# A two-block transformer on one core: inverses fetched in two transfers, three steps moved, two weight loads put later

## The chip, the cores and the metric

The kernel runs on one core of one Trainium2 chip. The metric is the device time of one execution in microseconds (us). It was run three times: median 2306.06 us, from 2299.68 to 2307.3. One further execution was taken by the profiler, and everything said of stages, lines and waits comes from that one.

The core has a matrix engine (TensorE; PE in the profile, its weight loads PEld), VectorE (DVE), ScalarE (ACT), GpSimd (POOL) and SyncE (SP). SyncE computes nothing here: it issues nearly all DMA transfers, in its program's order, and a transfer that has to wait for data holds up every later one on SyncE. Each engine works through its own instructions strictly in order.

## The reference

Everything is float32. The input x is 8 batch elements of 512 tokens by 256 features, with a condition vector per element and a context of 64 tokens by 192 features. Two transformer blocks follow each other.

```python
# block 0: 16 heads of 16
h = modulate(ln(x), shift_sa, scale_sa);  q, k = ln(heads(h)), ln(heads(h))
x = x + gate_sa * softmax(q k^T * scale) v
h = modulate(ln(x), ...);  x = x + gate_ca * (attention(h Wq, ctx) Wo + b)
h = modulate(ln(x), ...);  x = x + gate_ff * ((silu(h W1) * (h W3)) W2)
# block 1: 16 heads of 64, rotary position on q and k
x = attention(adaln(x), adaln(x)) Wo + b + x       # self-attention
x = attention(adaln(x), ln(context)) Wo + b + x    # cross-attention
x = gelu(adaln(x) W1 + b1) W2 + b2 + x
```

## The kernel before

All of x stays on the chip, one tile per batch element (`xs[b]`, 128 partitions by 4 by 256). Block 0 runs as cycles: `cycle(c)` lays the self-attention of element c beside the cross-attention of element c-1 and the feed-forward of element c-2. Block 1 runs stage by stage over the eight elements: self-attention (`slots`, in groups g = 0 to 3 of four heads), cross-attention (`cross`) and feed-forward (`feed_forward`). The order of every engine's instructions is the order in which these functions call each other: they run inside `tc.manual_schedule`, so nothing there is reordered. Only what stands outside of it, such as the two weight loads at lines 1226 and 1227, may be placed elsewhere in an engine's order when the kernel is built.

**Turned rows.** Matrix products need the normalized rows with the features on the partitions. A norm has three pieces: statistics of two row tiles each (twice, line 182 on; the second ends with `rstd` on GpSimd, line 158) and the application (line 191). Then `blocks_turned` (line 410) turns 32 by 32 blocks on VectorE (413), writes them to DRAM with four transfers (416, `turned_d`) and reads them back with one (418, into z). `modulated` (427) scales and shifts on ScalarE. A function `turn` calls it, some steps later. `add_row` (448) adds a bias row to x on GpSimd.

**Softmax denominators.** `sums` multiplies the exponentials by ones on TensorE, ScalarE copies the sums out (`den`), and SyncE sends them to DRAM and back so that they lie one per lane (`rec`; lines 1093 and 1095, or 1307 and 1309). `inverse` takes the reciprocal on VectorE, stores it (1101 or 1316) and fetches it back repeated over 64 partitions (`rb`; 1106 with 4 transfers, 1321 with 8, of 128 KB each). `scaled` multiplies by it on VectorE and GpSimd (1112 or 1328).

**Cross-attention of block 1.** `cross` starts with six queries, then has places j = 0 to 7 for each element b. At j = 0 and 4 come a `sums` and a `score`; at every j one `queries` call, six ahead: two products of 512 columns, and a rotation on VectorE (868, 869) that empties one of four PSUM banks used in rotation (`ps_D`, `ps_O`, two `ps_X`), and at every second j two sums on GpSimd (873, 874). At j = 0 and 1 `outer` multiplies the values by the output weights. For the element before: `scaled` for its first half at j = 0, `inverse` for its second half at j = 1, `scaled` at j = 4, and the output products `cross_out` at j = 5 to 7. At j = 1 `turn` modulates the next element's rows; at j = 2 keys and values of the next element are fetched; at j = 4, 5, 6 the three pieces of the norm of element b + 2 run (`rows_`), the last with `blocks_turned` and `add_row`; at j = 6, behind them, `inverse` for this element's first half. Element 0 has neither `outer` nor `cross_out` nor `scaled` among its places, so it is short.

**Weights.** `load_w` fetches 1 MB into one of the places of a pool. `ff_w1` goes to where `ca_wv4` was, `ff_w2` to where `sa_wo` was, which TensorE reads until the end of self-attention (`last_out`). Their first use is `up(0, ...)` in the last element of cross-attention, or the feed-forward.

Of the kernel before, what the change touches and what calls it, by code (L numbers as in the profile page):

```python
# [10 lines left out]
F32 = mybir.dt.float32  # L11
I32 = mybir.dt.int32
AF = mybir.ActivationFunctionType
ALU = mybir.AluOpType
# [3 lines left out]
B, N, D, H, T, CD, FF = 8, 512, 256, 16, 64, 192, 1024  # L18
P = 128
# [25 lines left out]
def fast_path(ctx: ExitStack, tc: tile.TileContext, a: dict, out: bass.AP):  # L45

    nc = tc.nc
# [71 lines left out]
    def row(name):  # L119
        lo, hi = _ROWS[name]  # L120
        return rows[:, lo:hi]
# [88 lines left out]
    wk = sa0.enter_context(tc.tile_pool(name="sa0", bufs=2, side="right"))  # L210
# [421 lines left out]
    class CrossAttention:  # L632
# [22 lines left out]
        def blocks(self):  # L655
            turned_blocks0(self)
# [144 lines left out]
    def cycle(c):  # L801

        s, nxt, prev = sa[c], of(sa, c + 1), sa[c - 1]
        x, done = ca[c - 1], of(ca, c - 2)
        up, down = of(ff, c - 2), of(ff, c - 3)
        keys = [lambda p=p: keys1(p) for p in range(NPAIR)] if c == 1 else [lambda: None] * NPAIR
        store = store_keys1 if c == 1 else lambda g: None
        late = [up.turn] if c == 2 else []
        soon, then = ([x.turn], []) if c == 1 else ([], [x.turn])
        rows2, rows3 = ([] if c < n else [s.blocks] for s, n in ((x, 2), (up, 3)))  # L810

        scores, values = of_self(s, 0)
# [4 lines left out]
        group(scores, [keys[2], lambda: store(0), lambda: down.down(1), lambda: x.prepare(0), lambda: x.prepare(1),  # L817
                       *([up.turn] if c > 2 else []), lambda: up.up(0), lambda: x.prepare(2), *rows2, keys[3], lambda: up.up(1)],
              [lambda: s.queries_keys(2), lambda: s.back(0), *soon, lambda: nxt.norm(2)], values)
# [173 lines left out]
    with tc.tile_pool(name="ph4", bufs=2, reuse_waits="tile") as wk:  # L993
# [4 lines left out]
        def by_way():  # L998
            return wk.tile([P, 2, N], F32, tag="t", name="t")

        class Batch:
# [6 lines left out]
            def norm(self, n):  # L1008
                self.pieces[n]()
                if n == 2:  # L1010
                    self.s["raw"] = blocks_turned(by_way(), self.s["z"])
                    add_row(self.b, row("sabo"))

            def turn(self):
                self.s["hT"] = modulated(rows_tile(nk), self.s["raw"], self.b, a1, b1)
# [81 lines left out]
            def inverse(self, g):  # L1097
                rec = self.s["rec", g]
                nc.vector.reciprocal(rec, rec)
                d = dram.tile([4, N], F32, tag="rec_d", name="rec_d")  # L1100
                nc.sync.dma_start(flat(d), rec)
                check(rec)
                for u in range(2):
                    self.s["rb", g, u] = rb = wk.tile([P, N], F32, tag="rb", name="rb", bufs=3)
                    for e in range(2):
                        nc.sync.dma_start(rb[64 * e : 64 * e + 64, :],
                                                d[2 * u + e : 2 * u + e + 1, :].to_broadcast([64, N]))

            def scaled(self, g):
                o = self.s["oT", g]  # L1110
                for u, eng in enumerate((nc.vector, nc.gpsimd)):
                    eng.tensor_tensor(o[:, u, :], o[:, u, :], self.s["rb", g, u], ALU.mult)

            def last_out(self, ks):
                s = self.s
# [16 lines left out]
        class First:  # L1132
# [4 lines left out]
            def norm(self, n):  # L1137
                self.pieces[n]()
                if n == 2:
                    first_rows.append(blocks_turned(by_way(), first_rows.pop()))  # L1140
                    add_row(0, row("cabo"))

            def turn(self):
                first_rows.append(modulated(rows_tile(nk), first_rows.pop(), 0, a1, b1))
# [3 lines left out]
        def slots():  # L1148
# [9 lines left out]
            for b, this in enumerate(todo):  # L1158
                nxt = todo[b + 1] if b + 1 < B else First()
                last = todo[b - 1] if b else None  # L1160
                for g in range(NG):
# [34 lines left out]
                    if before:  # L1196
                        before[0].scaled(before[1])
                    this.sums(g)
                    before = this, g
            end = todo[-1]  # L1200
            cross_values(wk, 1)
# [21 lines left out]

    extra.extend([bank_d, bank_o])
    with tc.tile_pool(name="ph5", bufs=2, reuse_waits="tile") as wk:
        w_f1 = load_w("ff_w1", 1)
        w_f2 = load_w("ff_w2", 3)
        kvs.append((wk.tile([P, NPAIR, T], F32, name="kb", bufs=1), wk.tile([P, NPAIR, 2, T], F32, name="vb", bufs=1)))


# [80 lines left out]
        def inverse(b, half):  # L1311
            s = ss[b]
            rec = s["rec", half]
            nc.vector.reciprocal(rec, rec)
            rd = dram.tile([4, 2, N], F32, tag="rec5", name="rec5")
            nc.sync.dma_start(flat(rd), rec)
            check(rec)
            for j in range(4):
                s["rb", j] = rb = wk.tile([P, N], F32, tag="rb", name="rb", bufs=4)
                for e in range(2):  # L1320
                    nc.sync.dma_start(rb[64 * e : 64 * e + 64, :], rd[j, e : e + 1, :].to_broadcast([64, N]))  # L1321

        def scaled(b, half):
            s = ss[b]
            for j in range(4):
                p = 4 * half + j
                pr = s["p", p // 2][:, p % 2, :]
                (nc.gpsimd, nc.vector)[p % 2].tensor_tensor(pr, pr, s["rb", j], ALU.mult)

        def out_tile(b, t, lhsT, w):  # L1330
            s = ss[b]
# [52 lines left out]
            return good  # L1384

        def cross():
            LEAD = 6
            held = [bank_s() for _ in range(2)]
            for n in range(LEAD):
# [4 lines left out]
            for b in range(B):  # L1394
                for j in range(NPAIR):
# [24 lines left out]
                    if j == 2 and b + 1 < B:  # L1420
                        load_kb(b + 1)
                        load_vb(b + 1)
                    if 3 < j < 7:
                        rows_(b + 2, j - 4)
                    if j == 6:
                        if b == B - 1:
                            sums(b, 1)
# [890 lines left out]
```

## Time and profile before

| | |
|---|---|
| median of 3 runs | 2306.06 us |
| the profiled execution | 2305.44 us |
| its span, first to last instruction | 2303.6 us |
| mean granted TensorE clock | 0.990 |
| TensorE busy | 2265.9 us, 98% |
| VectorE, GpSimd, ScalarE busy | 1124.5, 922.9, 865.9 us |
| DMA: bytes moved | 115.69 MB, mean 50 GB/s |
| rb<-rec_d, transfers | 128 of 128 KB (block 1 self-attention) |
| rb<-rec, transfers | 128 of 128 KB (block 1 cross-attention) |

Times are counted from the first instruction. Block 0 lasts to about 800 us, the self-attention of block 1 to 1751.5, its cross-attention to about 2069 and the feed-forward to the end. A line of the timeline has start, length, engine, line of the kernel, operation, output and inputs, and in brackets how long the engine was idle before it and what ended that wait. A "landing" is the time at which the last part of a transfer told that it had arrived.

### The profile page before, as it was taken

The numbers are of one execution on the slowest core, as the hardware profiler recorded it, in microseconds if no ns is written. First come the engines' busy times: TensorE is split into PE (matmuls) and PEld (weight loads), VectorE is DVE, ScalarE is ACT, GpSimd is POOL, SyncE is SP. The second block draws the span as 40 slices with busy tenths as digits, with TensorE's granted clock in tenths as the row PEclk, the third lists the DMA queues.
The fourth block names the chain that finished last, engine by engine and source line by source line (L and its number), as shares of the span: only waits on it lengthen the run. The fifth ranks groups of instructions, "written<-read, shape, count | busy, mean of one in ns | idle before, by whom it ended". The sixth has DMA issues, their size and how long they took to land.

```text
span 2303.6 us, 30880 instructions
## 1 busy us (share of the span) xinstructions
PE 2265.9 (98%) x12092; PEld 1145.7 (50%) x12092; DVE 1124.5 (49%) x1946; ACT 865.9 (38%) x1309; POOL 922.9 (40%) x584
## 2 busy tenths in 40 slices
PE   9999999999999999999999999999999899999999
PEld 4444554544545633535353535353535456567666
DVE  5676666665555345353535353545453555442220
ACT  4666455555542133342434242424241121221222
POOL 4652333333200056464646464645453444431110
PEclk9999999999999999999999999999999999999999
DMA  6120110101102001010101010101033333332221
GB/s 192 34 94 22 49 28 21 49 7 43 44 10 76 19 15 38 20 38 20 38 20 38 20 38 20 38 20 38 20 97 106 85 105 92 100 90 70 55 63 35
DMA packets 119819, 115.69 MB, mean 50 GB/s; under 512 B 40065, under 2 KB 93041, under 8 KB 119665
## 3 DMA queue, kind: packets, MB, share of 16 engines
q1 hardware_dynamic: 118800, 111.01, 16.9%
q8 instruction: 97, 1.59, 0.3%
q0 software_dynamic: 576, 2.10, 0.2%
q10 hardware_dynamic: 288, 0.52, 0.1%
q14 instruction: 58, 0.47, 0.1%
HBM read 85.73 MB, written 27.86 MB: 49 GB/s over the span
## 4 chain that ended last, share of the span: by engine, by line
PE 88%; DMA 4%; DVE 3%; SPq 2%; POOL 1%; issue 1%; ACT 0%; DVEq 0%; POOLq 0%; ACTq 0%
PE ps_P L88 40%; PE ps_B L88 30%; PE ps_S L88 5%; PE ps_D L88 4%; PE ps_X L88 4%; PE ps_O L88 2%; SPq L1321 1%; DMA rb<-rec 1%; DMA rec<-rec 1%; DMA turned_d<-hT 1%; PE ps_B L566 1%; SPq L416 1%; DVE z L191 1%; POOL var L557 1%; PE ps_B L598 1%
## 5 line engine op out<-in xcount | busy, mean ns | idle before, releaser
L615 ACT ACTIVATE p<-ps_B 128x512 f32<-128x512 f32 x576 | 291.6, 624 | 162.3 <-PE ps_B L88 162.2
L1058 ACT ACTIVATE p<-ps_P 128x1024 f32<-128x1024 f32 x256 | 244.9, 1025 | 90.0 <-PE ps_P L88 89.8
L88 PE MATMUL ps_P<-q,k 32*128 32x512 f32 x2048 | 238.9, 600 | 1.4 <-DVE t L1037 1.4
L1067 POOL TENSOR_TENSOR sm<-sm,p 128x1024 f32<-128x1024 f32 x64 | 176.9, 2764 | 135.3 <-ACT p L1058 134.7
L88 PE MATMUL ps_B<-hT,w 128*128 128x512 f32 x512 | 226.9, 597 | 1.4 <-ACT hT L407 0.9
L88 PE MATMUL ps_P<-p,v 128*32 128x512 f32 x2048 | 226.4, 594 | 0.0
L1026 ACT COPY v<-ps_P 128x1024 f32<-128x1024 f32 x32 | 32.4, 1012 | 375.8 <-PE ps_P L88 375.8
L1067 DVE TENSOR_TENSOR sm<-sm,p 128x1024 f32<-128x1024 f32 x64 | 101.6, 1588 | 145.3 <-ACT p L1058 145.3
L88 PEld LDWEIGHTS ps_P<-q,k 32*128 32x128 f32 x2048 | 99.1, 184 | 139.2 <-issue 113.6
L88 PEld LDWEIGHTS ps_B<-hT,w 128*128 128x128 f32 x512 | 95.3, 190 | 127.5 <-issue 97.0
L158 POOL TENSOR_TENSOR rstd<-rstd,mhalf 128x4 f32<-128x4 f32 x49 | 52.4, 1069 | 260.3 <-DVE rstd L157 259.1
L88 PE MATMUL ps_B<-q,k 16*128 16x512 f32 x1024 | 146.2, 618 | 1.2 <-DVE k L570 1.2
L88 PEld LDWEIGHTS ps_P<-p,v 128*32 128x32 f32 x2048 | 63.3, 110 | 158.3 <-issue 134.8
L1065 POOL TENSOR_TENSOR sm<-p 128x1024 f32<-128x1024 f32 x32 | 79.2, 2475 | 152.6 <-ACT p L1058 152.6
L557 POOL TENSOR_TENSOR var<-var,mhalf 128x32 f32<-128x32 f32 (+1 forms) x17 | 87.8, 5164 | 105.8 <-DVE var L551 98.8
L1036 DVE TENSOR_TENSOR t<-ps_P,rope_c 128x1024 f32<-128x1024 f32 x64 | 78.4, 1225 | 95.8 <-POOL q L1040 55.9
L88 PE MATMUL ps_B<-p,h 128*32 128x512 f32 x1024 | 120.5, 610 | 0.0
L609 POOL TENSOR_TENSOR attn<-attn,gate 128x256 f32<-128x256 f32 x32 | 23.4, 732 | 241.1 <-DVE attn L607 240.0
L1065 DVE TENSOR_TENSOR sm<-p 128x1024 f32<-128x1024 f32 x32 | 39.2, 1225 | 162.5 <-ACT p L1058 162.5
L88 PE MATMUL ps_P<-hT,w_sa_wq 128*128 128x512 f32 x256 | 118.3, 605 | 0.0
L88 PE MATMUL ps_B<-w,hid 128*128 128x256 f32 x512 | 115.4, 385 | 0.0
L88 PE MATMUL ps_P<-hT,w_sa_wk 128*128 128x512 f32 x256 | 115.1, 592 | 0.0
(246 smaller groups left out, 3708.3 us busy)
## 6 DMA issues: line engine op xcount, KB each, us to landing
z<-turned_d SPq DMA_DIRECT2D x35, 512.0 KB
rb<-rec_d SPq DMA_DIRECT2D x128, 128.0 KB
rb<-rec SPq DMA_DIRECT2D x128, 128.0 KB
turned_d<-hT SPq DMA_DIRECT2D x104, 128.0 KB
turned_d<-t SPq DMA_DIRECT2D x36, 128.0 KB
out_dram<-x SPq DMA_DIRECT2D x15, 256.0 KB
x<-in_x_dram SPq DMA_DIRECT2D x7, 512.0 KB
gate<-modd SPq DMA_DIRECT2D x24, 128.0 KB
```

Of the source, the lines that this page charges most:

```text
L88: nc.tensor.matmul(o, lhsT, rhs, start=start, stop=stop)
L158: nc.gpsimd.tensor_tensor(r[:, :n], r[:, :n], mhalf[:, :n], ALU.pow)
L191: nc.vector.tensor_scalar(d[:, t, :width], x[:, t, :], s["mv"][:, t, 0:1], s["r"][:, t : t + 1], ALU.subtract, ALU.mult)
L416: nc.sync.dma_start(d[:, :, :, r, :].rearrange("a j k c -> j k a c"), flat_[32 * r : 32 * r + 32].rearrange("j (k a c) -> j k a c", k=2, a=4))
L557: nc.gpsimd.tensor_tensor(var, var, half, ALU.pow)
L609: nc.gpsimd.tensor_tensor(attn, attn, gate.to_broadcast([P, NT, 4, HD0]), ALU.mult)
L615: nc.scalar.activation(p[i], ps, AF.Exp, scale=HD0 ** -0.5)
L1026: nc.scalar.copy(s["v", half][:, t0 : t0 + 2, :], ps)
L1036: nc.vector.tensor_tensor(c, ps, rope_c[:, None, :].to_broadcast([P, 2, N]), ALU.mult)
L1058: nc.scalar.activation(pr, pss[u], AF.Exp, scale=HD1 ** -0.5)
L1065: eng.tensor_tensor(s["sm", g, u], s["p", g, 0, u], s["p", g, 1, u], ALU.add)
L1067: eng.tensor_tensor(s["sm", g, u], s["sm", g, u], s["p", g, kt, u], ALU.add)
```

## The change

Five edits. (1) `inverse` in both attentions of block 1 fetches `rb` as one tile with two transfers, one for each half of the partitions, in place of four of 128 KB (self-attention) or eight (cross-attention): the bytes stay the same. (2) The rows of self-attention in block 1 are turned by a function of their own, `blocks`, called behind `sums(1)` and no longer in the third piece of the norm; `add_row` stays there. (3) In block 0 `rows2`, the turning of the rows for cross-attention, stands behind `up.up(1)` in the cycle's list. (4) In `cross` the three pieces of `rows_` move from j = 4, 5, 6 to j = 3, 4, 5. (5) `ff_w1` and `ff_w2` are loaded at j = 3 of the second element (b = 1), within the order written out by hand, and no longer before the stage.

```diff
 # cycle(c), group 1
-  ... lambda: up.up(0), lambda: x.prepare(2), *rows2, keys[3], lambda: up.up(1)],
+  ... lambda: up.up(0), lambda: x.prepare(2), keys[3], lambda: up.up(1), *rows2],
 # class Batch (class First likewise, with first_rows and "cabo")
             def norm(self, n):
                 self.pieces[n]()
                 if n == 2:
-                    self.s["raw"] = blocks_turned(by_way(), self.s["z"])
                     add_row(self.b, row("sabo"))
+
+            def blocks(self):
+                self.s["raw"] = blocks_turned(by_way(), self.s["z"])
 # Batch.inverse
-                for u in range(2):
-                    self.s["rb", g, u] = rb = wk.tile([P, N], F32, tag="rb", name="rb", bufs=3)
-                    for e in range(2):
-                        nc.sync.dma_start(rb[64 * e : 64 * e + 64, :],
-                                                d[2 * u + e : 2 * u + e + 1, :].to_broadcast([64, N]))
+                self.s["rb", g] = rb = wk.tile([P, 2, N], F32, tag="rb", name="rb")
+                for e in range(2):
+                    nc.sync.dma_start(rb[64 * e : 64 * e + 64], d[None, e::2, :].to_broadcast([64, 2, N]))
 # slots
                     this.sums(g)
+                    if g == 1:
+                        nxt.blocks()
 # before the stage
-        w_f1 = load_w("ff_w1", 1)
-        w_f2 = load_w("ff_w2", 3)
+        w_f1 = w_f2 = None
 # inverse of cross-attention
-            for j in range(4):
-                s["rb", j] = rb = wk.tile([P, N], F32, tag="rb", name="rb", bufs=4)
-                for e in range(2):
-                    nc.sync.dma_start(rb[64 * e : 64 * e + 64, :], rd[j, e : e + 1, :].to_broadcast([64, N]))
+            s["rb"] = rb = wk.tile([P, 4, N], F32, tag="rb", name="rb", bufs=1)
+            for e in range(2):
+                nc.sync.dma_start(rb[64 * e : 64 * e + 64], rd[None, :, e, :].to_broadcast([64, 4, N]))
 # cross, at place j of element b
-                    if 3 < j < 7:
-                        rows_(b + 2, j - 4)
+                    if 2 < j < 6:
+                        rows_(b + 2, j - 3)
+                    if b == 1 and j == 3:
+                        w_f1 = load_w("ff_w1", 1)
+                        w_f2 = load_w("ff_w2", 3)
```

In both `scaled` functions the operand `rb` becomes the matching slice of the one tile; otherwise they are the same.

More of the change, by code (lines that the diff above doesn't have):

```diff
@@ L817, in cycle @@
         group(scores, [keys[2], lambda: store(0), lambda: down.down(1), lambda: x.prepare(0), lambda: x.prepare(1),
-                       *([up.turn] if c > 2 else []), lambda: up.up(0), lambda: x.prepare(2), *rows2, keys[3], lambda: up.up(1)],
+                       *([up.turn] if c > 2 else []), lambda: up.up(0), lambda: x.prepare(2), keys[3], lambda: up.up(1), *rows2],
               [lambda: s.queries_keys(2), lambda: s.back(0), *soon, lambda: nxt.norm(2)], values)
@@ L1111, in scaled @@
                 for u, eng in enumerate((nc.vector, nc.gpsimd)):
-                    eng.tensor_tensor(o[:, u, :], o[:, u, :], self.s["rb", g, u], ALU.mult)
+                    eng.tensor_tensor(o[:, u, :], o[:, u, :], self.s["rb", g][:, u, :], ALU.mult)
             def last_out(self, ks):
@@ L1139, in norm, with blocks @@
                 if n == 2:
-                    first_rows.append(blocks_turned(by_way(), first_rows.pop()))
                     add_row(0, row("cabo"))
+            def blocks(self):
+                first_rows.append(blocks_turned(by_way(), first_rows.pop()))
             def turn(self):
@@ L1327, in scaled @@
                 pr = s["p", p // 2][:, p % 2, :]
-                (nc.gpsimd, nc.vector)[p % 2].tensor_tensor(pr, pr, s["rb", j], ALU.mult)
+                (nc.gpsimd, nc.vector)[p % 2].tensor_tensor(pr, pr, s["rb"][:, j, :], ALU.mult)
         def out_tile(b, t, lhsT, w):
@@ L1386, in cross @@
         def cross():
+            nonlocal w_f1, w_f2
             LEAD = 6
```

## Prediction, made before the result was known

> **What bounds the kernel now.** The page comes first. TensorE decides almost everywhere, so only the time in which it idles, or runs at half clock, can be won.
>
> ```profile
> span 2303.6 us, 30880 instructions
> PE 2265.9 (98%) x12092; PEld 1145.7 (50%) x12092; DVE 1124.5 (49%) x1946; ACT 865.9 (38%) x1309; POOL 922.9 (40%) x584
> ```
>
> Since busy matmul time is modelled, I read it by stretches next: length, then busy time of PE, PEld, DVE, ACT and POOL, granted clock, DMA share, GB/s. I cut at the end of block 1's self-attention (1751.5) and at each cross-attention element.
>
> ```profile
> 800.00:1751.50 951.50, 950.14 (x5681) 421.17 (x5681) 448.40 (x500) 340.19 (x372) 501.46 (x275) 1.00 0.12 36
> 1751.50:1791.50 40.00, 35.35 (x145) 15.81 (x143) 17.60 (x28) 8.21 (x11) 15.25 (x13) 0.91 0.21 47
> 1791.50:1839.70 48.20, 39.28 (x193) 22.94 (x192) 24.38 (x52) 8.70 (x12) 23.75 (x18) 0.93 0.34 90
> 1839.70:1878.07 38.37, 37.43 (x193) 22.52 (x192) 19.93 (x42) 8.81 (x12) 18.36 (x14) 1.00 0.37 99
> ```
>
> Self-attention of block 1 leaves PE 1.4 us idle in 951.5: nothing to win there. An undisturbed element is 37.4 us of PE. The first element (cut at 1791.5) idles 4.65 us, the second 8.92, the next five 0.94, 1.97, 1.04, 2.07 and 1.02 (the last four from the same view, not shown). The start of the feed-forward idles 0.79 more. Sum: 21.4 us. The waits of PE name the causes (total, times, longest):
>
> ```profile
> PE ps_D L88 <- DVE t L869: 13.9, 6, 6.8
> PE ps_X L88 <- DMA kv<-v_d: 4.6, 1, 4.6
> PE ps_X L88 <- ACT hT L427: 2.1, 1, 2.1
> ```
>
> For the 13.9 us, the chain of waits of a later element (start, length, what):
>
> ```profile
> 1839.10 0.33 SPq L418
> ...
> 1839.46 3.28 DMA rec<-rec
> ...
> 1847.18 3.10 DMA rb<-rec
> ...
> 1850.98 0.68 DVE t L868
> ...
> 1852.41 1.96 PE ps_D L88 x4
> ```
>
> SyncE holds the store of the inverses (L1316) until it has got past the turned rows (L418), then takes 4.96 us to issue eight transfers (L1321 from 1842.81 in the timeline); VectorE stands in `scaled` (L1328) until the last lands, the rotation of a query behind it comes late, and PE lacks the bank.
>
> Last, the clock, by stretches:
>
> ```profile
> 1754.22:1757.63 3.41, 0.89 (x3) 0.06 (x1) 1.79 (x3) 0.00 (x0) 1.05 (x1) 1.00 1.15 306
> 1757.63:1764.45 6.82, 4.69 (x8) 2.81 (x9) 0.00 (x0) 0.59 (x1) 1.43 (x2) 0.50 0.27 38
> 1808.83:1815.65 6.82, 3.20 (x4) 1.17 (x4) 3.93 (x8) 0.00 (x0) 3.75 (x3) 0.50 0.12 36
> ```
>
> After the two long gaps the granted clock is 0.50 for 6.82 us; what PE does in it takes twice as long. That costs half of the 4.69 us busy, 2.35, and 39.28 - 37.43 = 1.85 in the second element. With the idle time 25.6 us can be won at most.
>
> **Step 1, weights out of the opening.** SyncE's order there (start, length):
>
> ```profile
> 1743.22 0.55 SPq L140 DMA_DIRECT2D w_ff_w<-in_ff_w_dram  x1
> 1745.70 0.38 SPq L989 DMA_DIRECT2D v_d<-v  x1
> 1751.71 0.38 SPq L140 DMA_DIRECT2D w_ff_w<-in_ff_w_dram  x1
> 1752.15 1.25 SPq L977 DMA_DIRECT2D kv<-v_d  x2
> ```
>
> The first 1 MB load goes ahead of the store v_d<-v, which lands 6.44 us after its issue by the chain; another such store took 2.6 us alone (landing mark, issue 1716.93). The second waits for PE's last read of `sa_wo` and then goes ahead of kv<-v_d, which lands 6.84 us after its issue; the like load at 1777.46 took 3.0 and 4.0. Without the two: v_d<-v issued near 1744.5 (two issues fewer ahead of it, by step 2), landed by 1749, kv by 1754, and PE wants it at 1755.1, when its second query ends. The 4.65 us go, and with them the half clock, 2.35: **7.0 us**. Next late would be v_d<-v; if it lands as slowly as its slowest row (4.34), 1 us is left.
>
> **Step 2, two transfers for eight (four in self-attention).** One of the eight takes 0.6 us of SyncE whatever its form: the issues of L416 and L977, with more and shorter rows, take 0.62 to 0.67. So 4.96 becomes 1.25. The row for two 256 KB transfers is missing. Bounds: each lands 2.9 us after its issue, as 128 KB does (end 3.5 after the first issue), or they move like the 512 KB of z<-turned_d, 3.5, behind the second issue (4.1). Old: 7.5. I take 4.1, the nearer in bytes. A loss is excluded as long as they use all engines (rival 3).
>
> **Step 3, norms one j sooner.** In the code the norm's pieces go from j = 4, 5, 6 to 3, 4, 5: the same VectorE work (4 statistics, 4 applications of 0.35, a transpose of 1.25), `rstd` and `add_row` on GpSimd (1.0, 2.4) and five DMAs, all past one query and in later elements one output tile. SyncE's order stays: rows, then inverse. On GpSimd `rstd` comes right behind the multiplications of j = 4 and `add_row` behind a query's sums; nothing asks for either soon. In an undisturbed element, counted from its first matmul: the query of j = 5 ends at 21, rotation, norm and transpose at 25, the last L416 at 28, z is issued at 30 and lands at 33.4; VectorE's reciprocal stands at 31, so rec lands behind z at 33.5 and rb, by step 2, at 37.7. `scaled` asks at 37.4 + 6.2 = 43.6 (6.2 from 1839.70 to the end of the rotation before it). 6 us of slack, so the five gaps go, 0.94 + 1.97 + 1.04 + 2.07 + 1.02 = **7.0 us**, and the 0.79 of the feed-forward, whose last rb lands 3.4 sooner. GpSimd is next: 18.4 of 37.4 us busy, so it hides the move.
>
> The second element is not cured, for the first has no output tiles to cover anything. Normalized rows start after the rotation at 1789.47 instead of 1791.52, 2.05 sooner. The whole chain shifts: z lands 2.05 sooner and the 2.08 us wait for L427 goes. rec<-rec, still behind z<-turned_d, lands at 1800.7; rb at 1804.8 instead of 1810.1; two multiplications (1.4) and 1.4 until PE has its bank: 1807.6. PE ends its query at 1803.5: a gap of 4.1 stays of 8.9, 4.8 won. Half clock: gaps of 3.77 (at 693), 4.65 and 6.84 were followed by 6.8 us of it, 2.08 was not. So I expect it and charge 2.4, between nothing and 3.2 (6.39 us busy at 0.50 after the gap at 693, halved), against 1.85 now: **4.2 us** net. The Trainium skill, "TensorE: Matmul & The Clock Gate", Part 1, lets the clock halve after an idle window of about 3.4 us, with windows that run freely. By that a 4.1 us gap would hold a whole idle window only by luck of phase, and the sum would be 2.4 lower. The trace speaks against so strict a reading: the stretch 1754.22 to 1757.63 had 0.89 us of PE work, and 0.50 followed.
>
> **Step 4, the loads in the second element.** 1.0 us of SyncE and 2 MB, behind keys and values of the next element. The DMA engines reached 306 GB/s (stretch above), and 245 for the 1.5 MB from the second w_ff to kb, landed in 6.4 us: 7 to 9 us. Behind them on SyncE and its queue stand the element's own sums (den<-den, then rec<-den, which holds SyncE until they land) and the turned rows. Counted without the opening's 7 us, the sums land at 1823 to 1825, the reciprocal starts 0 to 1.6 us late on VectorE, with only rotations behind it, rb lands by 1837, and `scaled` asks at 1839. Forecast 0; bounds 0 and 8 (rival 1).
>
> **Step 5, turned rows behind sums.** Block 0: the transpose moves behind `up(1)`, two VectorE instructions, 1.3 us; L427 starts 2.5 to 4.7 us after z lands and ACT never idles before it. Block 1: blocks (one transpose, five DMAs) wait behind den_d<-den and its landing, 2 us; L427 has 6 us (1.8 in the first batch, where 0.3 may show on ACT, not on PE). den_d<-den goes 4.7 us sooner, and nothing asked for it. 0; without the slack 2 us a batch. The shorter rb of self-attention: VectorE and GpSimd waited once each for it (1.9, 2.5), under 14 us of PE's last products. 0.
>
> **Sum.** 7.0 + 4.2 + 7.0 + 0.8 = 19.0. The profiled execution took 2305.44 (span 2303.6), so 2286.4; the median shown is 0.6 above it: 2287.
>
> **Rivals.**
> 1. *The loads cost a gap.* If the 2 MB take 12.6 (twice the 6.3 of one), the second element's inverses land some 4 to 5 us late and a gap with half clock (3.2) comes between second and third: 8 us back, **2295**. For it: v_d<-v and kv<-v_d were held up in just this way. Against: a whole element lies between.
> 2. *Another wait takes the place.* VectorE and GpSimd work in order; if `rstd` or `add_row`, now beside `scaled`, holds the multiplications, or the compiled order still puts a load ahead of kv<-v_d, most gaps re-form: **2304**. Against: both are half idle in these elements, and SyncE's order is written out by hand where the loads now stand.
> 3. *Slower: the transfers land late.* Were the two spread over fewer engines by their inner row count (2 in self-attention), 128 KB at 306/16 = 19 GB/s an engine would take 3.4 us, two of them 7, a pair near 9 with latency. It decides from 9.7 us after the first issue on: rb is issued at 996.8 and read at 1006.5. A few us beyond, at half weight for VectorE's idle half, are 1 to 2 us in 31 groups: 30 to 60, **2345**. Against: both sides begin with 64 partitions, as the small ones do, and z<-turned_d moves 512 KB in 3.5. The Trainium skill, "DMA: Bandwidth & Descriptors", has the slowest dimension of both sides choose the engines; by that 64 gives all 16, and the time stays 2287.
>
> **Numbers.** Forecast 0.70 (own range 2279 to 2292: low, no half clock and rec not behind z; high, 1 us left in the opening and 4 in the second element), rival 1 0.14, rival 2 0.09, rival 3 0.07. The range 2278 to 2297 holds the first two. 0.3% is 6.9 us, about what a measurement can tell from no change: faster 0.84, same 0.09, slower 0.07.
>
> **What would show it.** Right: no wait for kv<-v_d, clock 1.00 from 1751 on; L1321 two issues of 0.6; no wait of VectorE for rb from the third element on; one gap near 4 us left in the second. Wrong: rb landing over 5 us after its issue (step 2), elements still above 38 us (step 3), a gap at the third element (step 4), any new wait of PE before 1751 (step 5).

## The result, and the profile after

The changed kernel takes **2295.21 us** (median of 20 runs, 2291.03 to 2306.25), the kernel before beside it 2303.2 (20 runs). By the medians that is 8.0 us faster, where 19 were forecast. The ratio is 0.9967, with an interval from 0.9956 to 0.9978, which is 7.6 us. The profiled execution took 2293.24 us. The page after, its first lines:

```profile
span 2291.4 us, 30655 instructions
PE 2252.5 (98%) x12092; PEld 1138.9 (50%) x12092; DVE 1138.4 (50%) x1946; ACT 864.9 (38%) x1309; POOL 938.4 (41%) x584
```

TensorE lost 13.4 us of busy time, which a change that moves only waits should not give; of that below. VectorE and GpSimd got busier, by 13.9 and 15.5 us, with as many instructions: something makes them slower.

The stretches after (the first three elements of cross-attention, cut at the same TensorE instructions as before; columns as before):

```profile
1741.00:1773.76 32.76, 32.76 (x146) 14.65 (x144) 18.34 (x29) 8.21 (x11) 15.28 (x13) 1.00 0.11 24
1773.76:1825.44 51.68, 39.57 (x194) 22.69 (x193) 28.17 (x51) 8.69 (x12) 25.91 (x18) 0.90 0.56 135
1825.44:1864.24 38.80, 37.72 (x193) 22.44 (x193) 23.56 (x42) 8.81 (x12) 20.34 (x14) 1.00 0.46 98
```

The opening is cured: 32.76 us for 40.00, TensorE without a pause, clock 1.00. The second element is worse, 51.68 for 48.20, and idles 12.1 us. The third is worse too, 38.80 for 38.37. Its DMA share went from 0.37 to 0.46 at the same 98 to 99 GB/s: the same bytes now cost more engine time. The waits of TensorE after:

```profile
PE ps_D L88 <- DVE t L869: 10.0, 1, 10.0
PE ps_D L88 <- POOL p L1330: 6.8, 11, 2.0
```

The six waits for the rotation have become one long one, in the second element, and a new row stands there: TensorE waits eleven times for GpSimd's multiplication by `rb` (L1330). The wait for kv<-v_d is gone. The chain of waits around the end of the third element has two fetches of inverses, first the one for the first half of an element, then the one for its second half:

```profile
1860.11 3.35 DMA rec<-rec
...
1863.54 0.62 SPq L1323
...
1864.20 6.93 DMA rb<-rec
...
1871.83 1.76 DVE p L1330
...
1877.21 7.03 DMA rb<-rec
```

The two issues are 0.62 us each, as forecast, but the second lands 6.93 us after it was issued, 7.6 after the first issue. The eight before had landed 7.5 us after theirs.

The second half's fetch is the one that TensorE meets, since its multiplications stand right ahead of the output products (`cross_out`). In the third element (timeline):

```profile
1845.29 1.89 PE L88 MATMUL ps_D<-vw,p 128*128 128x256 f32 x8
1845.88 3.46 POOL L1330 TENSOR_TENSOR p<-p,rb 128x512 f32<-128x512 f32 x2 [2.70 <-DMA rb<-rec]
1847.71 1.13 PE L88 MATMUL ps_D<-vw,p 128*128 128x256 f32 x4 [0.53 <-POOL p L1330]
1849.39 1.13 PE L88 MATMUL ps_D<-vw,p 128*128 128x256 f32 x4 [0.55 <-POOL p L1330]
```

The fetch was issued 12.6 us into the element (1838.00 less 1825.44) and had landed at 20.3; the output products begin at 19.9.

All stages together, as the time on TensorE from the start of one instruction to that of another, the same two in every trace (the order of its instructions is the same). The last three columns are experiments, told below.

| stage, us | before | after | edit 4 alone (e3) | after with eight transfers (e5) | after with four (e10) |
|---|---|---|---|---|---|
| start to the first cycles | 198.4 | 192.7 | 198.8 | 192.9 | 198.3 |
| block 0, cycles | 500.1 | 493.8 | 498.4 | 492.2 | 492.2 |
| end of block 0 | 103.6 | 104.5 | 103.5 | 104.4 | 104.5 |
| self-attention, block 1 | 948.0 | 948.6 | 948.0 | 951.7 | 948.2 |
| cross-attention, 1st element | 40.0 | 32.8 | 39.1 | 32.8 | 32.8 |
| 2nd element | 48.2 | 51.7 | 47.5 | 48.3 | 48.9 |
| 3rd to 7th element | 194.2 | 196.3 | 186.0 | 186.0 | 186.0 |
| start of the feed-forward | 35.7 | 35.3 | 34.5 | 34.5 | 34.5 |

Most of the first line is not the change's: in each profiled execution 3.4 to 17.1 us fall at half clock there (17.07 before, 3.41 after, but 17.07 again in e8, which has the changed kernel's block 0), so the two profiled times differ by 12.2 us where the medians, over many such starts, differ by 8.0. The 951.7 of e5 comes from the clock too: a wait of 1.9 us near 870 us, which the changed kernel has as well (1.4 before), was followed by 6.83 us at half clock in that execution.

### The profile page after: what moved, and what is told of

Its sections match the earlier page's. It is cut to its first block, busy times and chain, and to the rows that moved or that the text cites. A ratio compares the mean times of both kernels' runs of the same rounds, so it can differ in the third digit from the quotient of the medians.

```text
span 2291.4 us, 30655 instructions
## 1 busy us (share of the span) xinstructions
PE 2252.5 (98%) x12092; PEld 1138.9 (50%) x12092; DVE 1138.4 (50%) x1946; ACT 864.9 (38%) x1309; POOL 938.4 (41%) x584
## 4 chain that ended last, share of the span: by engine, by line
PE 83%; DMA 8%; DVE 5%; POOL 2%; issue 1%; SPq 1%; ACT 0%; DVEq 0%; POOLq 0%; ACTq 0%
PE ps_P L88 41%; PE ps_B L88 29%; DMA rb<-rec 5%; PE ps_S L88 4%; PE ps_X L88 3%; PE ps_D L88 2%; PE ps_O L88 2%; DMA rec<-rec 2%; DVE p L1330 1%; DVE z L191 1%; DMA turned_d<-hT 1%; PE ps_B L566 1%; SPq L416 1%; POOL var L557 1%; DVE t L868 1%
## 5 line engine op out<-in xcount | busy, mean ns | idle before, releaser
L88 PE MATMUL ps_B<-q,k 16*128 16x512 f32 x1024 | 140.1, 616 | 1.4 <-DVE k L570 1.4
```

The lines of the kernel that those rows point to most:

```text
L88: nc.tensor.matmul(o, lhsT, rhs, start=start, stop=stop)
```

## The experiments

Where a ratio is given, it is to the kernel before on the same chip, with its 95% interval.

**e1: edit 3 alone** (the turning of the cross-attention rows behind `up.up(1)` in block 0).

```diff
-  ... lambda: up.up(0), lambda: x.prepare(2), *rows2, keys[3], lambda: up.up(1)],
+  ... lambda: up.up(0), lambda: x.prepare(2), keys[3], lambda: up.up(1), *rows2],
```

> The kernel before with edit 3 alone (block 0: turned rows behind up(1)). Theory, from the starts of the same TensorE instruction in both profiles: four products of block 0 that work side by side wait 0.9 us in every cycle from the second on for banks that up(1) frees, and the busy time hides it; the edit frees them 1.3 us sooner: 6 cycles times 0.93, 5.6 us less, about 2297.6. Rival, the forecast's own term: nothing, 2303.

2297.56 us, ratio 0.9968 [0.9956, 0.9981]: 7.4 us faster by an edit that I had priced at nothing. The stretches of the cycles of block 0, before and then in this run:

```profile
199.85:699.92 500.07, 496.30 (x2648) 251.67 (x2645) 302.16 (x615) 265.56 (x504) 150.22 (x100) 0.99 0.11 29
```

```profile
194.31:688.13 493.82, 490.05 (x2648) 248.89 (x2645) 301.23 (x615) 265.03 (x504) 150.54 (x100) 0.99 0.11 29
```

Idle time is 3.77 us in both. What shrank is busy time. The timeline of one cycle, before:

```profile
261.06 1.25 DVE L413 STREAM_TRANSPOSE hT<-z 128x1024 f32<-128x1024 f32 x1
...
261.53 2.99 PE L88 MATMUL ps_B<-q,k 16*128 16x512 f32 x16
...
262.23 0.65 DVE L731 SCALAR_TENSOR_TENSOR t<-t,ps_B 128x512 f32<-128x512 f32 x1
...
262.98 0.69 DVE L732 TENSOR_TENSOR hid<-ps_B,t 128x512 f32<-128x512 f32 x1
```

and the same place with the edit:

```profile
255.40 0.68 DVE L731 SCALAR_TENSOR_TENSOR t<-t,ps_B 128x512 f32<-128x512 f32 x1
...
255.98 2.06 PE L88 MATMUL ps_B<-q,k 16*128 16x512 f32 x16
256.18 0.69 DVE L732 TENSOR_TENSOR hid<-ps_B,t 128x512 f32<-128x512 f32 x1
...
256.79 1.24 DVE L413 STREAM_TRANSPOSE hT<-z 128x1024 f32<-128x1024 f32 x1
```

The same sixteen products take 2.99 us behind the transpose and 2.06 without it. VectorE empties two banks of `ps_B` with L731 and L732; while the transpose stands ahead of them, some of these products wait for a bank (a weight load of the group waits for L731 until 262.93). The pause lies inside the group, whose matmul ends are modelled, and counts as busy. The cycle's period falls from 90.10 us (261.53 to 351.63) to 89.17 (255.98 to 345.15): 0.93 in each of six cycles, 5.6 us, of which 0.8 comes back at the end of block 0. The Trainium skill, "Trainium Kernel Development and Optimization", Performance Expectations, calls matmul busy time a bad metric for how close a kernel is to roofline, because matmuls are pipelined. The trace agrees that it misleads: 2.99 against 2.06 us of "busy" for the same work.

One of the six cycles lies ahead of the table's second line. The other five give 4.6 of its 6.3 us, and 1.6 are half clock that the trace before has in the middle of the cycles, right behind one of these slow groups (351.63 to 354.62):

```profile
351.34:354.75 3.41, 3.41 (x19) 1.49 (x19) 2.33 (x3) 1.90 (x4) 2.28 (x1) 1.00 0.26 57
354.75:358.16 3.41, 3.41 (x20) 1.76 (x22) 2.54 (x8) 1.14 (x3) 0.17 (x1) 0.50 0.49 109
```

Of the five traces with the old order (before, e2, e3, e4, e6) four have such a fall behind a slow group, of the nine with the new order none. So the hidden wait seems to cost clock as well; no run takes the two apart.

**e2: edit 5 alone** (the two loads at j = 3 of the second element).

```diff
-        w_f1 = load_w("ff_w1", 1)            # before the stage
-        w_f2 = load_w("ff_w2", 3)
+                    if b == 1 and j == 3:    # in cross()
+                        w_f1 = load_w("ff_w1", 1)
+                        w_f2 = load_w("ff_w2", 3)
```

> The kernel before with edit 5 alone (two weight loads in the second element). Theory: the opening of cross-attention gains 7.2 us (no wait for keys and values, no half clock), and the second element loses little: 2296. Rival: the 2 MB stand ahead of the second element's sums, so that it or the third gets a wait of its own of 3 us or more: 2299 or above.

2297.43 us, ratio 0.9971 [0.9957, 0.9985]. The first element takes 32.97 us. The second:

```profile
1776.81:1826.91 50.10, 41.39 (x193) 23.47 (x192) 24.48 (x52) 8.69 (x12) 23.77 (x18) 0.86 0.47 128
```

The opening gives the 7.0 us of step 1 exactly. The second element takes 1.9 more than before, all of it half clock (13.65 us of it, for 6.83): its idle time is 8.71, for 8.92 before, and the clock falls at 1789.65, ahead of the loads (1808.64). The third takes 38.60: the loads cost no gap behind them.

**e3: edit 4 alone** (norms one place sooner, eight transfers).

```diff
-                    if 3 < j < 7:
-                        rows_(b + 2, j - 4)
+                    if 2 < j < 6:
+                        rows_(b + 2, j - 3)
```

> The kernel before with edit 4 alone (norms one j sooner, eight small transfers kept). Theory: the five waits of 0.9 to 2.1 us from the third element on go, 7.0 us, as the inverse is fetched long before it is used; the second element gains 0.4 at most, since the norm's application then stands beside sums of GpSimd and takes 3.3 instead of 1.7: 2296. Rival: the waits of 0.5 to 2.0 us for GpSimd in front of the output products, seen in the changed kernel, come from the norm's place: 2301.

2292.55 us, ratio 0.995 [0.9935, 0.9965], 3 us less than I had expected. The third element:

```profile
1836.80:1873.99 37.19, 37.19 (x194) 22.61 (x193) 22.68 (x42) 8.81 (x12) 18.52 (x14) 1.00 0.39 102
```

The third to seventh take 37.19 each without any pause, with all eight transfers still there. So the gaps of the later elements needed the sooner norms and nothing else. The second element hardly gains, 0.7.

**e4: edit 1 alone** (`rb` as one tile with two transfers, in both attentions; the cut shows cross-attention).

```diff
-            for j in range(4):
-                s["rb", j] = rb = wk.tile([P, N], F32, tag="rb", name="rb", bufs=4)
-                for e in range(2):
-                    nc.sync.dma_start(rb[64 * e : 64 * e + 64, :], rd[j, e : e + 1, :].to_broadcast([64, N]))
+            s["rb"] = rb = wk.tile([P, 4, N], F32, tag="rb", name="rb", bufs=1)
+            for e in range(2):
+                nc.sync.dma_start(rb[64 * e : 64 * e + 64], rd[None, :, e, :].to_broadcast([64, 4, N]))
```

> The kernel before with edit 1 alone (two transfers for eight, and for four). Theory: a fetch is 1 MB, twice what the forecast counted, and lands 7.6 us after its first issue as before; all multiplications start together after the last landing and VectorE and GpSimd slow each other (2.4 and 3.4 us for two instead of 1.4 and 2.5), so each element gets 2 to 3 us longer: 2303 + 15 = 2318. Rival, the forecast's own term: rb lands 3.4 us sooner, the waits of the elements go, 2297.

2343.24 us, ratio 1.0152 [1.0133, 1.0172]: 35 us slower, where I had expected 15. Self-attention is unchanged (948.0); every later element takes 42 to 45 us, and behind the second element the clock falls five times more, for 20.5 us in all. The waits of TensorE:

```profile
PE ps_D L88 <- DVE t L869: 22.8, 6, 8.4
PE ps_D L88 <- POOL p L1325: 11.1, 10, 3.8
```

and the chain of one element (L1318 issues the fetch):

```profile
1847.18 0.62 SPq L1318
...
1847.85 6.70 DMA rb<-rec
```

Issued at 1847.18, the inverses lie there at 1854.55; before, the first pair of eight lay there 3.6 us after its first issue, and the multiplications began with it while the rest was on its way. Now all four wait for the last byte. Here the fetch goes out 3.45 us into the element (1847.18 less 1843.73); in the changed kernel, with the norms sooner, 0.7 us ahead of it (1863.54 to 1864.24). That hides part of the price there, and none of it here.

**e5: the changed kernel with eight transfers again** (edits 2 to 5; the diff of e4 turned round, in self-attention too).

> The changed kernel with edit 1 undone (eight small transfers again, four in self-attention), edits 2 to 5 kept. Theory: elements three to seven take 37.2 us each as with edit 4 alone, where the changed kernel has 38.5 to 41.7 (10.4 us), the start of the feed-forward 34.5 (0.8), and the second element some 3 less: 14 us under the changed kernel, 2281. Rival: moving the norms and the loads together has a price of its own, so that the changed kernel's waits stay with eight transfers too: 2295.

2282.46 us, ratio 0.991 [0.9892, 0.9928]. The third element, without any pause:

```profile
1823.80:1860.99 37.19, 37.19 (x193) 22.61 (x193) 22.70 (x42) 8.80 (x12) 18.50 (x14) 1.00 0.39 102
```

One long wait is left in the stage, 6.7 us for the rotation in the second element. In the third, the second half's fetch goes out 12.1 us in (1835.90 less 1823.80), its first pair of transfers has landed 3.5 us later, and TensorE does not wait for the multiplications. Against the changed kernel that is 12.7 us by the medians, and 14.5 in the stages: 10.3 in the third to seventh element, 3.4 in the second, 0.8 in the feed-forward. **Edit 1 is the loss in this change.**

**e6: edit 2 alone** (rows of block 1's self-attention turned behind `sums(1)`).

```diff
-                    self.s["raw"] = blocks_turned(by_way(), self.s["z"])     # in norm
+                    if g == 1:                                               # in slots
+                        nxt.blocks()
```

> The kernel before with edit 2 alone (turned rows of self-attention behind the sums on SyncE). Theory: nothing of it lies on the path: 2303, and at most 0.6 us more within self-attention (948.0 before, 948.6 in the changed kernel). Rival: it is a share of the gain: 2300 or less.

2303.63 us, ratio 1.0002 [0.9986, 1.0017]: nothing, as forecast. Self-attention took 948.52 us for 948.02, with TensorE busy for 946.66 in both.

**e7: the changed kernel, `rb` of cross-attention read from separate rows.** It leaves the inverses out: 64 different rows of x lie in their place, so the fetch also does not wait for the store (`wide` is a view of x with a row of its own for each partition).

```diff
-                nc.sync.dma_start(rb[64 * e : 64 * e + 64], rd[None, :, e, :].to_broadcast([64, 4, N]))
+                nc.sync.dma_start(rb[64 * e : 64 * e + 64], wide[:, :, e, :])
```

> The changed kernel, but the two transfers of cross-attention read 64 rows of their own for the 64 partitions out of x, where the real ones read the same four rows 64 times; the bytes, the 2 KB pieces and the order are the same. The values multiplied with are therefore not the inverses, and the transfers don't wait for the store before them to land. It prices the landing alone. Theory 'the shared rows are slow': the second lands 5 us or less after the first issue and a piece takes about 84 ns. Theory 'the bytes are slow': 7.6 us and 150 ns as in the changed kernel.

One run, 2281.26 us. The two transfers land 5.3 to 6.9 and 7.0 to 8.6 us after their own issue by the landing marks, no sooner than in the changed kernel (5.0 to 5.3 and 6.7 to 7.1 from the third element on, in all fetches but one). That 64 partitions read one row is not what makes them slow. The elements take 37.2 to 37.3 all the same: SyncE does not wait for the store, so the fetch goes out earlier in the element (the third's second half 10.75 us in, for 12.56) and lands before the output products.

**e8: e5, and in the first element the rows of the third at j = 2, the first inverse at j = 5.**

```diff
-                    if 2 < j < 6:
+                    if 2 < j < 6 and b:
                         rows_(b + 2, j - 3)
+                    if b == 0 and j == 2:
+                        rows_(2, 2)
+                    if b == 0 and j == 5:
+                        inverse(0, 0)
...
-                        inverse(b, 0)
+                        if b:
+                            inverse(b, 0)
```

> As the changed kernel with eight transfers, and in the first element alone the rows of the third are normalized and turned at j = 2, and the inverse of the first half is taken at j = 5, so that both are through before the second element asks. Theory, that the second element waits for just these two chains: it takes 38 to 39 us instead of 48 to 52, without half clock; 2271. Rival: something else in the short first element (keys and values of the next, sums of its second half) holds it: 2281 as without.

2276.09 us, ratio 0.9878 [0.9859, 0.9897]: 28 us under the kernel before. The second element:

```profile
1777.06:1818.13 41.07, 38.35 (x194) 22.20 (x193) 24.20 (x48) 8.80 (x12) 21.40 (x17) 1.00 0.48 136
```

The second element is 7.2 us shorter than in e5 and never falls to half clock, so the order of the first element, of rows and inverse together, had left it late. I had expected 38 to 39 us there and 2271 in all. The second keeps waits of 1.81, 0.39 and 0.38 us, and the third and fourth take 38.5 and 37.8 in place of 37.2, so the two chains are most of the cause and not all of it.

**e9: e7's question for the width.** The two fetches go to all 128 partitions, two j each, in 4 KB pieces; as in e7, rows of x stand for the inverses.

```diff
-                nc.sync.dma_start(rb[64 * e : 64 * e + 64], rd[None, :, e, :].to_broadcast([64, 4, N]))
+                nc.sync.dma_start(rb[:, 2 * e : 2 * e + 2, :], wide[:, 2 * e : 2 * e + 2, :])
```

> The changed kernel, in which the two cross-attention fetches of 512 KB go to all 128 partitions each (two j per fetch, 4 KB per partition, read from 128 separate rows of x): it leaves out the inverses (rows of x stand in their place). Same bytes, same number of transfers, twice the partitions. If the bytes alone set the landing (1 MB), the last still lands 7.3 to 8.5 us after the first issue. If a destination of only 64 partitions is what limits (z, 512 KB to 128 partitions, landed in 3.5), the two land 3.5 to 4 and 4.5 to 5 us after the first issue.

One run, 2275.86 us. The same 1 MB lands 5.1 to 6.5 us after the first issue in the second halves, and 6.0 to 7.6 in the first halves, which run beside z (5.3 in the last). To twice 64 partitions it took 7.4 to 7.7 in nearly every element. The gain is 1 to 2 us, between the two expectations.

**e10: the changed kernel, `rb` as two tiles of two j, four transfers of 256 KB in the order of use.**

```diff
-            s["rb"] = rb = wk.tile([P, 4, N], F32, tag="rb", name="rb", bufs=1)
-            for e in range(2):
-                nc.sync.dma_start(rb[64 * e : 64 * e + 64], rd[None, :, e, :].to_broadcast([64, 4, N]))
+            for u in range(2):
+                s["rb", u] = rb = wk.tile([P, 2, N], F32, tag="rb", name="rb")
+                for e in range(2):
+                    nc.sync.dma_start(rb[64 * e : 64 * e + 64], rd[None, 2 * u : 2 * u + 2, e, :].to_broadcast([64, 2, N]))
```

> The changed kernel with rb of cross-attention as two tiles of two j each, fetched by four transfers of 256 KB in the order of use. Theory (bytes set the last landing, one tile makes all four multiplications wait for it): four issues of 0.62, first pair landed 4 to 4.5 us after the first issue, last 7.3 to 7.6; the first two multiplications start some 3 us sooner and no longer all at once, so the gaps of elements 3 to 7 shrink from about 2 us to under 0.7 and the kernel takes 2284 to 2288. Rival (only the number of transfers matters, the fewer the worse the packing of pieces): the first pair lands as late as before, elements stay at 38.6 and the time at 2295.

2283.88 us, ratio 0.9917 [0.9891, 0.9944]. By the landing marks the last of the four lands 6.9 to 8.5 us after the first issue, hardly sooner than with two or eight, and the first pair after 4.8 to 5.4, once 6.1 (I had expected 4 to 4.5). That is enough: the third to seventh element take 37.19 each, without a pause.

The multiplications of a first half on VectorE and GpSimd, here and then in the changed kernel (timeline):

```profile
1869.50 1.00 DVE L1331 TENSOR_TENSOR p<-p,rb 128x512 f32<-128x512 f32 x1
1870.82 0.69 DVE L1331 TENSOR_TENSOR p<-p,rb 128x512 f32<-128x512 f32 x1 [0.32 <-DMA rb<-rec]
...
1868.68 1.27 POOL L1331 TENSOR_TENSOR p<-p,rb 128x512 f32<-128x512 f32 x1 [7.64 <-DMA rb<-rec]
1870.89 1.76 POOL L1331 TENSOR_TENSOR p<-p,rb 128x512 f32<-128x512 f32 x1 [0.94 <-DMA rb<-rec]
```

```profile
1871.22 2.37 DVE L1330 TENSOR_TENSOR p<-p,rb 128x512 f32<-128x512 f32 x2 [0.77 <-DMA rb<-rec]
...
1871.28 3.45 POOL L1330 TENSOR_TENSOR p<-p,rb 128x512 f32<-128x512 f32 x2 [9.92 <-DMA rb<-rec]
```

With two tiles GpSimd begins at 5.3 us after the first issue and the last multiplication ends at 9.3; with one tile they begin at 7.7 and end at 11.2, and as both engines begin at once, they slow each other (last section). The second half, for which TensorE waits, gains alike: GpSimd begins 17.4 us into the third element (1843.59 less 1826.18) for 20.4 (1845.88 less 1825.44). So it is one tile, which makes every reader wait for the last byte, that turns a late landing into gaps.

**e11: e9 in pieces of 2 KB.** Each of the two fetches to 128 partitions takes every second j; rows of x stand for the inverses again.

```diff
-                nc.sync.dma_start(rb[64 * e : 64 * e + 64], rd[None, :, e, :].to_broadcast([64, 4, N]))
+                nc.sync.dma_start(rb[:, e::2, :], wide[:, e::2, :])
```

> As e9, with the two cross-attention fetches of 512 KB to all 128 partitions, but each takes every second j (0 and 2, then 1 and 3), so that its pieces are 2 KB as in the changed kernel and not 4 KB. It leaves out the inverses (rows of x stand in their place). If the width of 64 partitions is what slows a sustained fetch (2 KB in 150 ns), the pieces take 84 ns here and the last lands 5 to 6.5 us after the first issue where nothing runs beside it, as in e9. If the length of the pieces does, 2 KB take 140 to 170 ns as before and the last lands 7.4 or later.

One run, 2276.65 us. A piece of 2 KB takes 84 ns by the DMA packet records, and the last lands 5.8 to 6.3 us after the first issue in six of the eight second halves, beside which no z runs (8.1 and 8.2 in the other two). In the changed kernel the same pieces take 84 ns at first and 140 to 180 once the fetch is under way (median 158 in the fetch issued at 1863.54). Length of the pieces, shared rows (e7) and issuing are thus out: once under way, the fetch is slow since it goes to 64 partitions. 2 KB on 16 engines in 84 ns are 390 GB/s, in 158 ns 207.

**e12: e8 with the four transfers of e10.**

> e8 (the first element of cross-attention reordered) with the four transfers and two tiles of e10 in place of eight transfers. SyncE issues the inverses in 2.6 us instead of 5.0 and the first pair lands near 5.2 us after the first issue. Theory: the second element stays near 41 us, since its last gap hangs on the sums' landing and not on the fetch, the third and fourth (38.5 and 37.8 in e8) come nearer to 37.2: 2274 to 2276. Rival: the pairs land 1.5 us later than the first of eight and open a gap in the second element: 2278.

**2271.76 us**, ratio 0.9872 [0.9848, 0.9896], the best measured: 29 us under the kernel before by the ratio. The second element:

```profile
1773.72:1813.63 39.91, 37.97 (x194) 22.28 (x193) 23.85 (x48) 8.81 (x12) 23.17 (x17) 1.00 0.60 154
```

That is 2 us below what I expected, 1 us of it in the second element, where one wait of 1.7 for the rotation is left. The third takes 37.4.

## Why the prediction was right and wrong

- **Step 1, weights out of the opening: right.** 7.0 forecast, 7.0 in e2 and 7.2 after; no wait for kv<-v_d, clock 1.00.
- **Step 2, two transfers for eight: wrong, and this is the step that failed.** I sized the fetch wrongly: "two 256 KB transfers", put beside the 512 KB of z. That is the size in self-attention. In cross-attention eight of 128 KB are 1 MB, and the two are 512 KB each, as the page after says:

```profile
rb<-rec SPq DMA_DIRECT2D x32, 512.0 KB
```

  The term of 4.1 us from the first issue was 7.6. Of the 3.5 that I missed, the forgotten half of the bytes is about half (1 MB to 128 partitions lands after 5.8 to 6.3 in e11), and the width of 64 partitions the rest. Eight transfers were bound by SyncE, as I had read (4.96 of issuing and 3.1 for the last), but two exchange that bound for one as long. I had the bytes in my own table (128 transfers of 128 KB for 16 fetches). A second thing I did not weigh at all: one tile in place of four. I had excluded a loss "as long as they use all engines"; the loss came from the readers.

  It came at a place for which the working has no row, the second half of an element. By the term of 4.1 the third element's fetch would have landed 16.7 us in, ahead of the output products at 19.9; it landed at 20.3, and TensorE waited for GpSimd. In the third to seventh element such waits add up to 6.2 us. The longest, 1.97 in the seventh, behind a fetch that took 9.4 us, was followed by 3.41 us at half clock (41.7 us for that element, 38.5 to 38.8 for the others). With eight transfers or four there is none of them (e5, e10).
- **Step 3, norms one place sooner: right in what it wins, wrong in the slack.** With eight or four transfers the five gaps go entirely (194.2 to 186.0, 8.2 us for a forecast of 7.0), and the feed-forward gives 1.2 for 0.8. In the changed kernel too the five waits for the rotation are gone; the 194.2 became 196.3 by step 2's waits. But the slack of 6 us was not there. I had the first half's inverses landing 37.7 us into an element; they landed at 45.7 (1871.15 less 1825.44). Of these 8.0 us the fetch is 3.5. The other 4.5 lie ahead of it: the inverses' store reached DRAM at 38.0 for 33.5, as the turned rows were read back (z) at 34.3 for 30. The norm's application had been priced at four times 0.35; moved beside GpSimd's query sums it took 3.28:

```profile
1850.49 3.28 DVE L191 TENSOR_SCALAR z<-x,mv,rstd 128x256 f32<-128x256 f32 x4
```

  and the multiplications ahead of it waited for `rb` themselves, so that z was 1.3 us later than in e5 (33.0). I had asked whether GpSimd has time for the move, and not what it does to VectorE beside it. VectorE then waited 0.77 us for the first half's `rb` (1871.22), and TensorE still had its bank in time.
- **Step 3, the second element: wrong.** 4.2 won were forecast, 3.5 were lost. The rows started sooner but their norm took 3.28 instead of 1.71 (at 1771.64), which left about 0.5 of the 2.05 us; the store of the inverses, issued behind z at 1781.33, took until 1785.96, when the fetch went out; and this landed at 1793.6. The gap became 9.95 instead of 4.1. My charge for half clock after a gap was right to be there, and too small: 10.24 us, where 6.8 had been seen. Edit 4 alone gave the element 0.7 (e3); with edits 2 to 5 it stands at 48.3 (e5), as before.
- **Step 4, the loads in the second element: right.** The own sums of that element were late behind the 2 MB, as rival 1 feared: rec<-den, which waits for them, went out 7.9 us after their issue (1806.99 to 1814.90; before, 3.0). No gap came at the third element (e2, e5).
- **Step 5, turned rows: right in block 1, wrong in block 0.** "0" was 4.8 us of hidden waits won, and 7.4 us (4.4 to 10.1) by e1's ratio. I looked at when the rows are needed (2.5 to 4.7 us of slack) and not at what VectorE's transpose held up: two multiplications that free banks. Its trace was in the row 2.99 against 2.0 us for equal products, and I took the idle time, and half clock behind idle gaps, as all there was to win; the 3.41 us at half clock from 354.75 on stood in the trace too.
- **The sum.** 8.0 us came. The stages of the table, without the first, give 6.8: 7.2 from the opening, 6.3 from block 0's cycles (with 1.6 of half clock that e1's trace does not have either) less 0.9 at their end, 0.6 lost in self-attention, 5.6 lost in elements two to seven, 0.3 won in the feed-forward. The forecast had 7.0 for the opening, nothing for block 0 and 11.2 won in the elements. Of the rivals, the third came nearest: the transfers landed late, though by their bytes and their width, in cross-attention alone, where the sooner norms hid a part. In self-attention, where I had looked for its price, it cost nothing that shows. (Its sum was off as well: 128 KB at 19 GB/s take 6.9 us, not 3.4.) That the time meets rival 1's 2295 is luck, since its gap behind the loads did not come. The time lies in the range because a gain that I had not seen paid for part of a loss that I had not seen.

## What to carry to other kernels

Work out from its bytes and its width how long a fetch runs before you make fewer transfers of it: if issuing them takes no longer, nothing lands sooner, and one tile in place of several takes away the early start of its readers. Follow a changed transfer to all of its readers, not only to the one whose wait you want to remove. Price an instruction at its new place by rows in which its new neighbours run too, and ask of every moved vector instruction which PSUM banks are freed behind it. Idle time of TensorE is not all that can be won: compare the busy time of equal groups of products at different places.

## What the runs showed of the hardware

- **A long fetch to 64 partitions is slower than one to 128.** Its first pieces of 2 KB took 84 ns each; once it was under way they took 140 to 180, whether the 64 partitions read one row or 64 (e7). Those to 128 partitions stayed at 84 (e11). That is 207 GB/s on 16 engines at the median of 158 against 390, and 1 MB landed after 7.4 to 7.7 us against 5.8 to 6.3. The Trainium skill, "DMA: Bandwidth & Descriptors", Rules for kernel authors, asks for 128 partitions for the most bandwidth; the runs agree, and show what 64 cost.
- **VectorE and GpSimd slow each other, and the rows read like turns.** The multiplication by `rb` takes 0.69 us on VectorE and 1.27 on GpSimd with the other idle. When both begin at once, VectorE's first keeps its 0.69 and the next ones take 1.76 and 1.73: GpSimd's, from 1871.28, ends at 1873.04, and VectorE's, from 1871.83, at 1873.59, 0.55 later. The norm's application, four instructions, takes 1.38 alone and 3.28 beside GpSimd's sums. The rotation (L868), which reads one input from PSUM, keeps 0.68 beside a GpSimd multiplication (1873.51). The Trainium skill, "GPSIMD Engine Reference", Specifications, has the two share their SBUF interfaces, in contention where a VectorE instruction has two SBUF inputs or is in a 2-port mode. The rows agree for the multiplication and the rotation; none tells in which mode the norm's application runs.
- **Half clock does not need an idle window.** The window ahead of the second fall in cross-attention of the changed kernel, and the one behind it:

```profile
2001.60:2005.01 3.41, 1.31 (x5) 0.68 (x4) 3.12 (x6) 0.00 (x0) 3.08 (x2) 1.00 0.09 15
2005.01:2008.42 3.41, 3.00 (x6) 2.12 (x7) 3.38 (x7) 0.00 (x0) 3.07 (x4) 0.50 0.00 0
```

  TensorE was busy for 1.31 of the 3.41 us, with gaps of no more than 1.97, and 0.50 followed. Nor does busy time set a bound that the traces agree on. Counted on in steps of 3.413 us from each trace's falls, a window with 1.40 us of work was followed by full clock (e4, 1938.76 to 1942.17), one with 1.52 by 0.50 (e5, 868.79 to 872.20), and one with 3.41, filled by a group of products that waited for banks, by 0.50 too (351.34 above). The ends of matmuls are modelled, so busy time does not tell how much TensorE did. The "idle window" of the Trainium skill, "TensorE: Matmul & The Clock Gate", Part 1, which the prediction weighed, is too strict for these rows.
